# A quantizer's scratch moved into the gate product's PSUM banks, with PSUM split in two pairs and four banks

## The chip, the cores and the metric

The kernel runs on one core of a Trainium2 chip. The metric is the device time of one execution in microseconds, as the median over runs. The engines are named as in the profile: PE is TensorE (matmuls; PEld its weight loads), DVE is VectorE, ACT is ScalarE, POOL is GpSimd, SP is SyncE, which here issues the DMAs. SBUF is the working memory. PSUM is the memory that PE writes to; each of its 128 partitions has eight banks of 512 fp32 numbers.

## The reference

The input is x with four sequences of 2048 tokens and 256 channels; all numbers are fp32. Four layers follow, each added to x behind a layernorm of x:

```python
x = x + attn_a(layernorm(x))   # v times s/s, where s sums exp-features of q and k over a head
x = x + ffn(layernorm(x))
x = x + attn_b(layernorm(x))   # linear attention over the four sequences, unit-norm q and k, two gates
x = x + ffn(layernorm(x))      # the same FFN weights again

def fp4_quant_dequant(x):      # blocks of 16 along the last dim
    scale = max(max(abs(xb)) / 6, 1e-12)
    q = GRID[searchsorted(MID, abs(xb / scale))] * sign(xb) * scale   # 0 .5 1 1.5 2 3 4 6

def ffn(x):                    # w_gate, w_up: 704 x 256; w_down: 256 x 704
    xq = quant(x)
    h = silu(xq @ quant(w_gate).T) * (xq @ quant(w_up).T)
    return quant(h) @ quant(w_down).T
```

Attention A divides q and k by norms over the whole tensor, so sums over all of x are needed before any of its output is final.

## The kernel before

**Staging.** A first pass loads x, sums its Gram matrix on PE, and folds, centers, quantizes and transposes the weights. Then come 16 groups (`group(j)`), each of 128 positions in all four sequences, S = 4 tiles of 128 tokens. A group passes through attention A, the first FFN, attention B and the second FFN. Groups overlap: while one is in an FFN, others are in an attention.

**One FFN tile** (`ffn_tile`, 16 x 2 x 4 = 128 of them). PE makes gate and up products of the tile in two halves of 352 columns (L1448), each product in a bank of its own. ACT takes silu of the gate bank into the SBUF tile `sil` (L1469), and DVE multiplies with the up bank into `h` in SBUF (L1480). Then the inner quantizer `to_grid` runs: DVE takes block maxima and their reciprocals (`to_scales`, L384 and L385), DVE divides by scales (`over_scales`, L389, a first pass over 704 columns, into `qa`), ACT takes scaled absolute values (`to_steps`, L395, into the bf16 tile `qm`), and DVE makes two more passes (`to_sum`, L402, in `qa`; `from_sum`, L405, into `qm`). Meanwhile PE transposes the block maxima (L1287), ACT scales them into `sT` (L1295), and SP spreads them by six DMAs over the partitions of `hqT` (L1304). PE transposes `qm` (L1505), ACT copies the result back (L1516), and POOL multiplies it into `hqT` (L1524). PE makes the down product (L1561), which DVE adds to x (L336 or L1593). The last group's second FFN (`apart` false) applies the scales on POOL to `qa` before the transpose instead (L1271, L1538, L1550).

**Other users of PSUM.** `turn` transposes through a bank (L1155, drained by ACT at L1162); `project` fills a bank for attention A (drained by DVE, L1330) and for attention B (L1178, drained by ACT, L1656); the first pass uses banks for `fold`, `center`, the Gram sums (two banks, L575) and the transposes of weights (L805, L837).

**Order.** `Plan` takes each operation with an engine, a cost, a rank and the tiles that it reads and writes, and lays all of them in one static order: at every step the free engine takes the ready operation of lowest rank whose buffers can be had. `plan.buf("mm")` asks for any free tile of a pool; a tile is held from the operation that first touches it until the last one that does. Engines then run their instructions in that order, and wait for each other by semaphores. The rank of an operation is an offset written beside it plus an entry of `BEGIN`, a table of 16 groups by six stages: attention A, first FFN's input and tiles, attention B, second FFN's input and tiles. `port=True` tells the planner to keep DVE and POOL operations so marked apart. `order(seed)` adds a random number to every rank unless the seed is 0.

```python
plan.pool("mm", banks[:4])      # gate and up products; in the first pass folds, centers, sums
plan.pool("bank", banks[4:])    # all else
tiles("qa", 3, [P, FF], fp)     # the quantizer's fp32 scratch
```

Of the kernel before, what the change touches and what calls it, by code (L numbers as in the profile page):

```python
# [13 lines left out]
AF = mybir.ActivationFunctionType  # L14
# [4 lines left out]
P = 128  # L19
# [230 lines left out]
def kernel(  # L250
# [40 lines left out]
    def one(shape, name, pool=wp, dtype=F32):  # L291
        return pool.tile(shape, dtype, tag=name, name=name)

    banks = [one([P, 512], f"bank{i}", ps) for i in range(8)]
    xs_of = [one([P, S, D], f"x{i}", fp) for i in range(8)]


# [84 lines left out]
    def to_scales(src, amax, rs):  # L382

        nc.vector.tensor_reduce(amax, src, AX.X, ALU.max, apply_absolute_value=True)  # L384
        nc.vector.reciprocal(rs, amax)  # L385

    def over_scales(a, src, rs):

        nc.vector.scalar_tensor_tensor(  # L389
            blocks(a), over_blocks(rs), -6.0 * BELOW, src, ALU.mult, ALU.mult  # L390
        )

    def to_steps(m, a):

        nc.scalar.activation(m, a, AF.Abs, scale=UP)  # L395
# [5 lines left out]
    def to_sum(a, m):  # L401
        nc.vector.scalar_tensor_tensor(a, m, FLOOR, a, ALU.max, ALU.add)  # L402
# [9 lines left out]
    def tiles(name, n, shape, pool, dtype=F32):  # L412
        made = [one(shape, f"{name}{i}", pool, dtype) for i in range(n)]
        plan.pool(name, made)
        return made

    plan.pool("mm", banks[:4])
    plan.pool("bank", banks[4:])
    plan.pool("x", xs_of)
    tiles("turned", 6, [P, KC, GT], fp)  # L420

# [3 lines left out]
    tiles("qmx", 1, [P, S * D], fp, BF16)  # L425
    tiles("sx", 2, [P, 3, S * D // BLK], fp)
    tiles("sil", 2, [P, HF], fp)
    tiles("qa", 3, [P, FF], fp)

    tiles("qm", 4, [P, 6 * P], fp, BF16)  # L430

# [18 lines left out]
    def first_pass():  # L450
# [444 lines left out]

        def fold(at, dst, token, lhs):

            mm = plan.buf("mm")

            def pe():  # L900
                for c in range(KC):
                    nc.tensor.matmul(
                        mm.ap[:, c * P : (c + 1) * P],
                        lhs(c),
                        mapT[:, c, :],
                        start=True,
                        stop=True,
                    )

            op(  # L910
                "PE",
                0.6,
                at,
                pe,
                [(MAPT, 0), (WNAT, 0), (MK, "b")],
                [(mm, 0)],
            )
            op(
                "ACT",
                0.4,  # L920
                at + 1,
                lambda: nc.scalar.copy(dst, mm.ap[:, :D]),
                [(mm, 0)],
                [token],
            )

        def center(at, w, n, tokens, bias=None):

            mm = plan.buf("mm")

            def pe():
                for c in range(KC):
                    nc.tensor.matmul(
                        mm.ap[:, :n], ones, w[:, c, :], start=(c == 0), stop=(c == KC - 1)
                    )

            def dve():
                less, part = mm.ap[:, :n], -1.0 / D  # L940
                if bias:
                    less, part = bias[0], 1.0 / D
                    nc.vector.scalar_tensor_tensor(
                        less, mm.ap[:, :n], -1.0, less, ALU.mult, ALU.add
                    )
                for c in range(KC):
                    nc.vector.scalar_tensor_tensor(
                        w[:, c, :], less, part, w[:, c, :], ALU.mult, ALU.add
                    )

            op("PE", 0.2 + n / 290.0, at, pe, tokens, [(mm, 0)])
            us = 0.3 + n / 300.0 if bias else 0.2 + n / 450.0
            more = [(bias[1], 0)] if bias else []
            op("DVE", us, at + 2, dve, [(mm, 0)], tokens + more, port=bool(bias))
# [64 lines left out]
            "DVE", 0.3, FIRST + 1.0, take_sums, [(b, 0) for b in GRAM] + [("cross", 0)], [("part", 1)]  # L1019
        )  # L1020
        for c in range(KC):
            mm = plan.buf("mm")

            def weigh(c=c, mm=mm):
                if c == 0:
                    nc.tensor.matmul(mm.ap, g00, wqkA[:, 0, :], start=True, stop=True)
                else:
                    nc.tensor.matmul(mm.ap, g01, wqkA[:, 0, :], start=True, stop=False)
                    nc.tensor.matmul(mm.ap, g11, wqkA[:, 1, :], start=False, stop=True)

            op("PE", 1.0 + 0.9 * c, FIRST, weigh, [(G, c), (WQK, 0)], [(mm, 0)])

            def square(c=c, mm=mm):
                for t in range(2):
                    cols = slice(t * D, (t + 1) * D)
                    nc.vector.scalar_tensor_tensor(
                        prod[:, c, cols],
                        mm.ap[:, cols],
                        1.0,
                        wqkA[:, c, cols],  # L1040
                        ALU.mult,
                        ALU.mult,
                        accum_out=part[:, 3 + c, t : t + 1],
                    )

            op(
                "DVE", 0.95, FIRST, square, [(mm, 0), (WQK, 0)], [(PROD, c), ("part", 2 + c)]
            )

        tot = plan.buf("mm")  # L1050

        def total():
            for i in range(5):
# [55 lines left out]


    BEGIN = [
        (-203, -171, -228, -523, -223, -182),
        (30, 31, 72, 172, 140, 266),
        (171, 285, 220, 271, 350, 410),
        (190, 259, 249, 359, 435, 433),
        (280, 328, 329, 443, 489, 531),
        (307, 307, 368, 481, 553, 554),
        (401, 391, 470, 576, 469, 654),
        (518, 526, 518, 624, 554, 722),
        (558, 601, 599, 701, 465, 825),  # L1120
        (552, 581, 635, 689, 613, 817),
        (646, 729, 663, 820, 279, 916),
        (670, 507, 738, 839, 676, 977),
        (741, 808, 767, 897, 501, 969),
        (773, 805, 838, 931, 446, 1029),
        (844, 848, 859, 963, 879, 1776),
        (857, 886, 876, 1038, 88, 801),
    ]

    def group(j):  # L1130
# [304 lines left out]


        def ffn_tile(at, k, s, xqT):
            h, qa, qm, sh = (plan.buf(p) for p in ("h", "qa", "qm", "sh"))

            apart = (k, j) != (2, NJ - 1)  # L1440
            for half in range(2):
                cols = slice(half * HF, (half + 1) * HF)
                g, u, sil = plan.buf("mm"), plan.buf("mm"), plan.buf("sil")

                def hidden(g=g, u=u, cols=cols):
                    for bank, w in ((g, wgT), (u, wuT)):
                        for c in range(KC):
                            nc.tensor.matmul(  # L1448
                                bank.ap[:, :HF],
                                xqT.ap[:, c, s * P : (s + 1) * P],  # L1450
                                w[:, c, cols],
                                start=(c == 0),
                                stop=(c == KC - 1),
                            )

                op(
                    "PE",
                    2.38,
                    at + 2.4 * half,
                    hidden,  # L1460
                    [(xqT, 0), (xqT, 1)]
                    + [("wgu", i) for i in range(3 * half, 3 * half + 3)],
                    [(g, 0), (u, 0), (h, "place", half)],
                )
                op(
                    "ACT",
                    0.42,
                    at + 2.5 + 2.4 * half,
                    lambda g=g, sil=sil: nc.scalar.activation(  # L1469
                        sil.ap, g.ap[:, :HF], AF.Silu  # L1470
                    ),
                    [(g, 0)],
                    [(sil, 0)],
                    table="silu",
                )
                op(
                    "DVE",
                    0.44,
                    at + 3 + 2.4 * half,
                    lambda u=u, sil=sil, half=half: nc.vector.tensor_mul(  # L1480
                        h.ap[:, half * FB // 2 : (half + 1) * FB // 2, :BLK],
                        blocks(sil.ap),
                        blocks(u.ap[:, :HF]),
                    ),
                    [(u, 0), (sil, 0)],
                    [(h, half)],
                )
            to_grid(
                at + 6,
                h,  # L1490
                range(2),
                qa,
                qm,
                sh,
                {"amax": 1.32, "pass": 0.86, "abs": 0.74, "n": FF},
                qm if apart else None,
            )
            hqT = plan.buf("hqT")
            if apart:
# [333 lines left out]

    for j in range(NJ):
        group(j)
    order = plan.order(10)
    with tc.manual_schedule():
        for i in order:
            plan.ops[i]["fn"]()
# [56 lines left out]
```

## Time and profile before

| | |
|---|---|
| Time, median of 3 runs | 1520.65 us (1520.2 to 1521.12) |
| Profiled execution: its own time, given as the span from first to last instruction | 1516.3 us |
| What the median has beyond that span | 4.35 us |
| Instructions | 21213 |
| Granted TensorE clock, mean | 0.998 |
| Gate and up matmuls (L1448) | 2048, busy 641.3 us |
| Down matmuls (L1561) | 1536, busy 351.0 us |
| First and last hidden matmul (L1448) | 113.0 us, 1497.6 us |

The profile is of one execution. A group's line gives the source line, the engine, the operation, what is written and read, the count, the busy time and the mean duration of one, and behind the bar the idle time of the engine ahead of them with what ended most of it. In the timeline a line gives start, length, engine, line, operation and tiles; what stands in brackets is idle time and its releaser. Each fp32 matmul of the program shows as two records.

### The profile page before, as it was taken

To read this page: it belongs to the slowest core of one execution; us is meant where nothing else is said; L and a number is where in the kernel's file an instruction comes from. 1 tells how busy PE (TensorE), PEld (TensorE's weight loads), DVE (VectorE), ACT (ScalarE), POOL (GpSimd) and SP (SyncE) were. 2 spreads that over 40 slices of the span, in tenths; PEclk is the share of its full clock that TensorE was granted. 3 is DMA by queue.
4 is the path that set the end of the run, shared out by engine and by line. 5 is a ranking of instruction groups with operands and counts; after the bars stand their busy time and mean duration, and the time that the engine had idled before them with its cause. 6 is when DMAs were issued, how large, how long until landed. Compare 5 with 4: busy or idle time off the path is not lost.

```text
span 1516.3 us, 21213 instructions
## 1 busy us (share of the span) xinstructions
PE 1480.2 (98%) x6486; PEld 1041.9 (69%) x6486; DVE 1388.9 (92%) x2140; ACT 882.5 (58%) x1812; POOL 747.5 (49%) x782
## 2 busy tenths in 40 slices
PE   7989999999999999999999999999999999999999
PEld 6746666676767667767666666676666776677766
DVE  7899999989999999999999899899889998999986
ACT  6557666466646654654565755675566546565442
POOL 5344454364655445454354554643465435764532
PEclk9999999999999999999999999999999999999999
DMA  9302220222221122213222212122213131122221
GB/s 284 84 1 38 36 41 11 51 59 38 41 58 37 35 53 52 56 34 62 60 43 45 46 25 50 38 46 60 46 19 57 36 61 30 36 52 50 60 61 29
DMA packets 130226, 76.62 MB, mean 51 GB/s; under 512 B 9536, under 2 KB 129856, under 8 KB 130112
## 3 DMA queue, kind: packets, MB, share of 16 engines
q1 hardware_dynamic: 130112, 75.27, 24.2%
q8 instruction: 51, 0.84, 0.2%
q14 instruction: 63, 0.52, 0.1%
HBM read 18.09 MB, written 8.39 MB: 17 GB/s over the span
## 4 chain that ended last, share of the span: by engine, by line
PE 79%; DVE 13%; ACT 3%; issue 2%; DMA 2%; POOL 1%; SPq 0%; ACTq 0%; POOLq 0%; DVEq 0%
PE bank L1448 33%; PE bank L1561 19%; PE bank L1178 16%; PE bank L1155 4%; PE bank L575 3%; PE bank L1505 2%; DMA hqT<-sT 1%; DVE qa L389 1%; DVE qa L402 1%; DVE sh L384 1%; DVE h L1480 1%; DVE x L336 1%; DVE pp L1668 1%; DVE qm L405 1%; PE bank L1287 1%
## 5 line engine op out<-in xcount | busy, mean ns | idle before, releaser
L1448 PE MATMUL bank<-wguT,turned 128*128 128x352 f32 x2048 | 641.3, 461 | 0.8 <-DVE h L1480 0.8
L1448 PEld LDWEIGHTS bank<-wguT,turned 128*128 128x128 f32 x2048 | 378.6, 191 | 193.3 <-issue 11.7
L1524 POOL TENSOR_TENSOR hqT<-hqT,qm 128x768 f32<-128x768 f32 x124 | 223.9, 1810 | 332.1 <-ACT qm L1516 163.8
L1561 PE MATMUL bank<-wdT,hqT 128*128 128x256 f32 x1536 | 351.0, 380 | 3.1 <-POOL hqT L1524 2.2
L1561 PEld LDWEIGHTS bank<-wdT,hqT 128*128 128x128 f32 x1536 | 289.5, 190 | 61.1 <-issue 7.9
L395 ACT ACTIVATE qm<-qa 128x704 bf16<-128x704 f32 (+1 forms) x136 | 105.7, 782 | 115.0 <-DVE qa L389 103.5
L1469 ACT ACTIVATE sil<-bank 128x352 f32<-128x352 f32 x256 | 116.0, 457 | 70.3 <-PE bank L1448 64.1
L1480 DVE TENSOR_TENSOR h<-sil,bank 128x352 f32<-128x352 f32 x256 | 128.5, 509 | 21.7 <-ACT sil L1469 11.0
L402 DVE SCALAR_TENSOR_TENSOR qa<-qm,qa 128x704 f32<-128x704 bf16 (+2 forms) x136 | 139.0, 1022 | 9.9 <-ACT qm L395 9.8
L1776 POOL TENSOR_TENSOR pp<-vg,sc 128x1024 f32<-128x1024 f32 x64 | 133.1, 2095 | 22.9 <-DVE tok L1797 19.7
L389 DVE SCALAR_TENSOR_TENSOR qa<-sh,h 128x704 f32<-128x704 f32 x128 | 137.6, 1083 | 0.9
L405 DVE SCALAR_TENSOR_TENSOR qm<-qm,qa 128x704 bf16<-128x704 bf16 x124 | 129.8, 1048 | 4.4 <-POOL norms_f L363 0.5
L1516 ACT COPY qm<-bank 128x768 bf16<-128x768 bf16 x124 | 98.1, 795 | 59.3 <-PE bank L1505 56.7
L384 DVE TENSOR_REDUCE sh<-h 128x44 f32<-128x748 f32 x128 | 119.2, 931 | 4.2
L1271 POOL TENSOR_TENSOR qax<-qax,sx 128x1024 f32<-128x1024 f32 x32 | 71.4, 2231 | 100.6 <-DVE qax L405 74.7
L1178 PE MATMUL bank<-wqkB,turned 128*128 128x512 f32 x256 | 120.0, 595 | 0.8 <-ACT turned L1162 0.8
L1178 PE MATMUL bank<-wvz,turned 128*128 128x512 f32 x256 | 116.8, 595 | 1.7 <-ACT wdT L846 0.9
L1162 ACT COPY turned<-bank 128x512 f32<-128x512 f32 x160 | 87.2, 589 | 43.1 <-PE bank L1155 42.7
L1668 DVE TENSOR_TENSOR pp<-qk 128x1024 f32<-128x1024 f32 x64 | 81.8, 1279 | 7.1 <-ACT qk L1656 7.0
L342 ACT ACTIVATE dev<-x,norms_f 128x256 f32<-128x256 f32 x128 | 64.9, 507 | 29.8 <-DVE x L336 27.8
L1178 PEld LDWEIGHTS bank<-wvz,turned 128*128 128x128 f32 x256 | 46.7, 190 | 49.4 <-issue 42.7
L1675 DVE TENSOR_REDUCE sc<-pp 128x64 f32<-128x1024 f32 x64 | 77.8, 1215 | 1.3
(195 smaller groups left out, 2211.9 us busy)
## 6 DMA issues: line engine op xcount, KB each, us to landing
hqT<-sT SPq DMA_DIRECT2D x744, 64.0 KB
x<-in_L_attn_a_x_dram SPq DMA_DIRECT2D x23, 512.0 KB
out_dram<-x SPq DMA_DIRECT2D x64, 128.0 KB
hqT<-in_L_ffn_w_down_dram SPq DMA_DIRECT2D x2, 352.0 KB
hqT<-in_L_ffn_w_gate_dram SPq DMA_DIRECT2D x5, 128.0 KB
hqT<-in_L_ffn_w_up_dram SPq DMA_DIRECT2D x5, 128.0 KB
x<-in_L_attn_a_x_dram SPq DMA_DIRECT2D x4, 128.0 KB
pp<-in_L_attn_a_Wq_dram SPq DMA_DIRECT2D x2, 256.0 KB
```

The costliest lines, as they stand in the source:

```text
L384: nc.vector.tensor_reduce(amax, src, AX.X, ALU.max, apply_absolute_value=True)
L389: nc.vector.scalar_tensor_tensor(blocks(a), over_blocks(rs), -6.0 * BELOW, src, ALU.mult, ALU.mult)
L395: nc.scalar.activation(m, a, AF.Abs, scale=UP)
L402: nc.vector.scalar_tensor_tensor(a, m, FLOOR, a, ALU.max, ALU.add)
L405: nc.vector.scalar_tensor_tensor(a if to is None else to, m, FLOOR, a, ALU.max, ALU.subtract)
L1178: nc.tensor.matmul(bank.ap[:, :n], lhs.ap[:, c, s * P : (s + 1) * P], w[:, c, :], start=(c == 0), stop=(c == KC - 1),)
L1448: nc.tensor.matmul(bank.ap[:, :HF], xqT.ap[:, c, s * P : (s + 1) * P], w[:, c, cols], start=(c == 0), stop=(c == KC - 1),)
L1469: lambda g=g, sil=sil: nc.scalar.activation(sil.ap, g.ap[:, :HF], AF.Silu),
L1480: lambda u=u, sil=sil, half=half: nc.vector.tensor_mul(h.ap[:, half * FB // 2 : (half + 1) * FB // 2, :BLK], blocks(sil.ap), blocks(u.ap[: ...
L1524: lambda: nc.gpsimd.tensor_mul(hqT.ap, hqT.ap, qm.ap.rearrange("p (c n) -> p c n", n=P)),
L1561: nc.tensor.matmul(o.ap[:, :D], hqT.ap[:, i, :], wdT[:, i, :], start=(i == 0), stop=(i == 5),)
L1776: nc.gpsimd.tensor_mul(pv.ap.rearrange("p t (n e) -> p t n e", e=HD), vg.ap[:, :, :D].rearrange("p t (n e) -> p t n e", e=HD), over_blocks ...
```

## The change

PSUM is divided anew: two pairs of adjacent banks (`pair`) and four single banks (`bank`); the pool `mm` is gone. A tile's two gate halves go to the two banks of one pair. Its up halves, and what else used `mm`, go to the four single banks. The inner quantizer no longer calls `to_grid`: it has its own copies of the same five steps, which use the pair as scratch in place of `qa` (704 columns across both banks, and 44 for the reciprocals), so the pair is held until `from_sum`. Those DVE operations are no longer marked `port`. `qa` falls from three tiles to two; in the groups only the last group's second FFN still uses it. The table of ranks is new, and the order is taken without random numbers. No arithmetic instruction is added or removed.

```diff
@@ -291,7 +291,8 @@
     def one(shape, name, pool=wp, dtype=F32):
         return pool.tile(shape, dtype, tag=name, name=name)
 
-    banks = [one([P, 512], f"bank{i}", ps) for i in range(8)]
+    pairs = [one([P, 2, 512], f"pair{i}", ps) for i in range(2)]
+    banks = [one([P, 512], f"bank{i}", ps) for i in range(4)]
     xs_of = [one([P, S, D], f"x{i}", fp) for i in range(8)]
 
 
@@ -414,8 +415,8 @@
         plan.pool(name, made)
         return made
 
-    plan.pool("mm", banks[:4])
-    plan.pool("bank", banks[4:])
+    plan.pool("pair", pairs)
+    plan.pool("bank", banks)
     plan.pool("x", xs_of)
     tiles("turned", 6, [P, KC, GT], fp)
 
@@ -425,7 +426,7 @@
     tiles("qmx", 1, [P, S * D], fp, BF16)
     tiles("sx", 2, [P, 3, S * D // BLK], fp)
     tiles("sil", 2, [P, HF], fp)
-    tiles("qa", 3, [P, FF], fp)
+    tiles("qa", 2, [P, FF], fp)
 
     tiles("qm", 4, [P, 6 * P], fp, BF16)
 
@@ -895,7 +896,7 @@
 
         def fold(at, dst, token, lhs):
 
-            mm = plan.buf("mm")
+            mm = plan.buf("bank")
 
             def pe():
                 for c in range(KC):
@@ -928,7 +929,7 @@
 
 
 
-            mm = plan.buf("mm")
+            mm = plan.buf("bank")
 
             def pe():
                 for c in range(KC):
@@ -1019,7 +1020,7 @@
             "DVE", 0.3, FIRST + 1.0, take_sums, [(b, 0) for b in GRAM] + [("cross", 0)], [("part", 1)]
         )
         for c in range(KC):
-            mm = plan.buf("mm")
+            mm = plan.buf("bank")
 
             def weigh(c=c, mm=mm):
                 if c == 0:
@@ -1047,7 +1048,7 @@
                 "DVE", 0.95, FIRST, square, [(mm, 0), (WQK, 0)], [(PROD, c), ("part", 2 + c)]
             )
 
-        tot = plan.buf("mm")
+        tot = plan.buf("bank")
 
         def total():
             for i in range(5):
@@ -1109,22 +1110,22 @@
 
 
     BEGIN = [
-        (-203, -171, -228, -523, -223, -182),
-        (30, 31, 72, 172, 140, 266),
...
-        (844, 848, 859, 963, 879, 1776),
-        (857, 886, 876, 1038, 88, 801),
+        (-765, -488, -607, -512, -538, -479),
+        (50, -442, -240, 262, -219, 287),
...
+        (836, 812, 859, 960, 1010, 1933),
+        (863, 308, 878, 1046, 300, 567),
     ]
 
     def group(j):
@@ -1435,18 +1436,19 @@
 
 
         def ffn_tile(at, k, s, xqT):
-            h, qa, qm, sh = (plan.buf(p) for p in ("h", "qa", "qm", "sh"))
+            h, g, qm, sh = (plan.buf(p) for p in ("h", "pair", "qm", "sh"))
+            qa = plan.buf("qa") if (k, j) == (2, NJ - 1) else None
 
             apart = (k, j) != (2, NJ - 1)
             for half in range(2):
                 cols = slice(half * HF, (half + 1) * HF)
-                g, u, sil = plan.buf("mm"), plan.buf("mm"), plan.buf("sil")
-
-                def hidden(g=g, u=u, cols=cols):
-                    for bank, w in ((g, wgT), (u, wuT)):
+                u, sil = plan.buf("bank"), plan.buf("sil")
+
+                def hidden(u=u, cols=cols, half=half):
+                    for bank, w in ((g.ap[:, half], wgT), (u.ap, wuT)):
                         for c in range(KC):
                             nc.tensor.matmul(
-                                bank.ap[:, :HF],
+                                bank[:, :HF],
                                 xqT.ap[:, c, s * P : (s + 1) * P],
                                 w[:, c, cols],
                                 start=(c == 0),
@@ -1460,16 +1462,16 @@
                     hidden,
                     [(xqT, 0), (xqT, 1)]
                     + [("wgu", i) for i in range(3 * half, 3 * half + 3)],
-                    [(g, 0), (u, 0), (h, "place", half)],
+                    [(g, half), (u, 0), (h, "place", half)],
                 )
                 op(
                     "ACT",
                     0.42,
                     at + 2.5 + 2.4 * half,
-                    lambda g=g, sil=sil: nc.scalar.activation(
-                        sil.ap, g.ap[:, :HF], AF.Silu
+                    lambda sil=sil, half=half: nc.scalar.activation(
+                        sil.ap, g.ap[:, half, :HF], AF.Silu
                     ),
-                    [(g, 0)],
+                    [(g, half)],
                     [(sil, 0)],
                     table="silu",
                 )
@@ -1485,15 +1487,52 @@
                     [(u, 0), (sil, 0)],
                     [(h, half)],
                 )
-            to_grid(
+            def flat():
+                return g.ap.rearrange("p t n -> p (t n)")
+
+            def a_and_m():
+                return flat()[:, :FF], qm.ap[:, :FF]
+
+            def rs():
+                return flat()[:, FF : FF + FB]
+
+            def hidden_scales():
+                to_scales(h.ap, sh.ap[:, 0, :], rs())
+
+            def hidden_over_scales():
+                over_scales(flat()[:, :FF], h.ap[:, :, :BLK], rs())
+
+            op(
+                "DVE",
+                1.32,
                 at + 6,
-                h,
-                range(2),
-                qa,
-                qm,
-                sh,
-                {"amax": 1.32, "pass": 0.86, "abs": 0.74, "n": FF},
-                qm if apart else None,
+                hidden_scales,
+                [(h, 0), (h, 1)],
+                [(sh, 0), (g, 0), (g, 1)],
+            )
+            op(
+                "DVE", 0.88, at + 7, hidden_over_scales, [(h, 0), (h, 1)], [(g, 0), (g, 1)]
+            )
+
+            def hidden_steps():
+                a, m = a_and_m()
+                to_steps(m, a)
+
+            def hidden_grid():
+                a, m = a_and_m()
+                from_sum(a, m, m if apart else qa.ap)
+
+            op("ACT", 0.74, at + 8, hidden_steps, [(g, 0), (g, 1)], [(qm, 0)])
+            op(
+                "DVE", 0.88, at + 10, lambda: to_sum(*a_and_m()), [(qm, 0)], [(g, 0), (g, 1)]
+            )
+            op(
+                "DVE",
+                0.88,
+                at + 10.1,
+                hidden_grid,
+                [(g, 0), (g, 1)] + ([] if apart else [(qm, 0)]),
+                [(qm if apart else qa, 0)],
             )
             hqT = plan.buf("hqT")
             if apart:
@@ -1833,7 +1872,7 @@
 
     for j in range(NJ):
         group(j)
-    order = plan.order(10)
+    order = plan.order(0)
     with tc.manual_schedule():
         for i in order:
             plan.ops[i]["fn"]()
```

More of the change, by code (lines that the diff above doesn't have):

```diff
@@ L1111 @@
     BEGIN = [
-        (-203, -171, -228, -523, -223, -182),
-        (30, 31, 72, 172, 140, 266),
[L1114 to L1125, printed above, removed]
-        (844, 848, 859, 963, 879, 1776),
-        (857, 886, 876, 1038, 88, 801),
+        (-765, -488, -607, -512, -538, -479),
+        (50, -442, -240, 262, -219, 287),
+        (183, 283, 216, 300, -429, 413),
+        (182, -98, 227, 358, 290, 440),
+        (269, 382, 228, 444, 501, 531),
+        (359, -27, 367, 453, 551, 553),
+        (413, 440, 467, 576, 644, 647),
+        (515, 301, 519, 290, 467, 728),
+        (559, 607, 599, 662, 614, 826),
+        (556, 583, 635, 683, -236, 818),
+        (643, 734, 655, 1018, -402, 221),
+        (676, -469, 747, 850, 844, 988),
+        (740, 743, 773, 899, 300, 972),
+        (772, 773, 840, 931, -244, 1033),
+        (836, 812, 859, 960, 1010, 1933),
+        (863, 308, 878, 1046, 300, 567),
     ]
```

## Prediction

> **What bounds the kernel now.** I read the page's busy shares first, to see which engines have room.
>
> ```profile
> span 1516.3 us, 21213 instructions
> PE 1480.2 (98%) x6486; PEld 1041.9 (69%) x6486; DVE 1388.9 (92%) x2140; ACT 882.5 (58%) x1812; POOL 747.5 (49%) x782
> ```
>
> PE has nearly no idle time and DVE little; ACT and POOL are half empty. A busy PE hides small gaps, so I went to the trace's matmuls and took the interval from each start to the next. Summing, over all shapes, the lower quartile of a shape's interval (295 ns for the 128x352 hidden matmul, 215 ns for 128x256, 429 ns for 128x512, 55 ns for a bf16 transpose) gives 1454.8 us, PE's issue floor. The excess over it is 49.2 us. With 9.2 us before the first matmul and 3.5 us behind the last start that makes the span, to a few tenths. By hundreds of us the excess is 6.3, 9.2, 2.9, 3.3, 2.9, 1.1, 1.4, 2.0, 3.0, 5.7, 0.8, 2.6, 1.2, 0.9, 5.3 and 0.7. So **at most 49 us (3.2%) can be gained by any reordering**, and a quiet stretch already loses only about 1 us in 100.
>
> Next, the windows view: the middle and the end of the span.
>
> ```profile
> 1200.00:1450.00 250.00, 249.47 (x1106) 179.76 (x1105) 233.37 (x333) 132.77 (x267) 124.16 (x102) 1.00 0.25 48
> 1450.00:1516.00 66.00, 59.52 (x278) 45.02 (x276) 47.79 (x68) 24.55 (x52) 21.11 (x18) 1.00 0.17 40
> ```
>
> The columns are stretch, length, then busy us of PE, PEld, DVE, ACT and POOL, granted clock (full) and DMA. PE is saturated late in the middle and not in the tail.
>
> Then the groups of instructions: the quantizer's three passes over the hidden tile, and GpSimd's multiplication.
>
> ```profile
> L402 DVE SCALAR_TENSOR_TENSOR qa<-qm,qa 128x704 f32<-128x704 bf16 (+2 forms) x136 | 139.0, 1022 | 9.9 <-ACT qm L395 9.8
> L389 DVE SCALAR_TENSOR_TENSOR qa<-sh,h 128x704 f32<-128x704 f32 x128 | 137.6, 1083 | 0.9
> L405 DVE SCALAR_TENSOR_TENSOR qm<-qm,qa 128x704 bf16<-128x704 bf16 x124 | 129.8, 1048 | 4.4 <-POOL norms_f L363 0.5
> L1524 POOL TENSOR_TENSOR hqT<-hqT,qm 128x768 f32<-128x768 f32 x124 | 223.9, 1810 | 332.1 <-ACT qm L1516 163.8
> ```
>
> The means hide two populations. The medians are 884, 886 and 892 ns, the longest 2.6 us. Sorted by whether a GpSimd instruction ran beside them, the passes average 871, 885 and 888 ns alone, and 1183, 1321 and 1249 ns beside one. The timeline near the end shows what that does to PE:
>
> ```profile
> 1456.06 3.89 POOL L1524 TENSOR_TENSOR hqT<-hqT,qm 128x768 f32<-128x768 f32 x2
> 1456.13 2.32 DVE L402 SCALAR_TENSOR_TENSOR qa<-qm,qa 128x704 f32<-128x704 bf16 x1 [1.33 <-ACT qm L395]
> 1458.48 2.21 DVE L405 SCALAR_TENSOR_TENSOR qm<-qm,qa 128x704 bf16<-128x704 bf16 x1
> 1460.75 0.51 PE L1505 MATMUL bank<-ident,qm 128*128 128x128 bf16 x6 [1.70 <-DVE qm L405]
> ```
>
> Two passes that take 0.88 us alone took 4.5 together beside GpSimd, and PE sat idle 1.70 us behind them. The rows with one operand in PSUM do not stretch: the 256 products h<-sil,bank never exceed 524 ns, and average 508 ns beside GpSimd against 514 alone.
>
> **The change, part by part.**
>
> *1. The three passes move to a PSUM pair.* Each then has one SBUF and one PSUM input, like h<-sil,bank. Taken at their time alone they save 128 x (1083 - 885) = 25.3 us, 128 x (1040 - 884) = 20.0 us (1040 is the mean of the 704-wide form) and 124 x (1048 - 888) = 19.8 us: **65 us of DVE**, from 1389 to 1324 (92% to 87%). No row of this trace writes PSUM from DVE, so I bound the price of the three passes and the reciprocal, four instructions a tile. From above: vz<-bank,norms_a,bvz at 512 elements takes 727 ns against 682 for pp<-pp alone, 45 ns more; 128 x 4 x 45 = 23 us. From below: behind x<-x,bank at 256 the next DVE instruction starts after 331 ns, behind tok<-pp after 342 (medians where DVE did not wait); 11 ns less, a gain of 6 us. I take zero: h<-sil,bank at 515 ns lies on the line through the SBUF-only rows (417 at 256 elements, 682 at 512, hence 516 at 352), and it is the nearest row.
>
> [...]
>
> *2. ACT and GpSimd.* The step pass (L395, 790 ns from SBUF) reads PSUM instead. L1516 copies 768 elements from PSUM in 795 ns, per element 729 ns for 704: between 0 and -8 us of ACT in all; I take zero, since ACT is at 58%. GpSimd's multiplication has a median of 1647 ns against its mean of 1810, so up to 124 x 0.163 = 20 us of GpSimd time goes too. Neither is on the path by itself; if their cover went, those sums are what they would give or cost.
>
> *3. PSUM is split anew.* Up products (u), and the first pass's folds, centers and sums, go to the four general banks. From first matmul to end of drain, what uses those banks now adds up to 373 us of transposes, 346 of attention A, 293 of Q, K, V and gates, 201 of scales, 222 of hidden transposes and 709 of down and output projections: 2144 us, over some 1400 us 1.5 banks of four. The u halves add 256 x 5.7 = 1459 us: 2.6 of four. That leaves room on average, less in bursts.
>
> [...]
>
> *4. The pair is held longer than a bank was.* Today a gate bank is free after silu, 3.1 us on average from its first matmul. Now the pair stays taken to the end of from_sum. Pairing the n-th tile's first hidden matmul with the n-th from_sum, I find today 10.7 us at the least, 26.7 at the median and 27.6 on average, with one tile every 10.84 us. So 2.5 tiles are in flight, and two will be allowed. In 96 of 126 cases tile n+2 starts today before tile n's from_sum has ended. Queued behind such a wait on PE is everything that comes after the hidden matmuls; for that reason the order has to change, and the new ranks do that. The sum for one undisturbed tile is 4.78 (PE) + 0.46 + 0.51 + 0.93 + 0.43 + 0.88 + 0.79 + 0.88 + 0.88 = 10.5 us, which agrees with the 10.7; the other 17 us are queueing on DVE. They must fall under 21.7 - 10.5 = 11.2 us. With 65 us less in DVE's queue, and PE able to take projections and down products in between (as much of PE as the hidden matmuls), I take it that they do.
>
> *5. First pass.* The Gram sums hold two of the four general banks, so folds and centers turn over in two instead of six; PE is covered there by the Gram matmuls (40.15 us busy in the first 50). Two qa tiles instead of three serve eight weight quantizations; their last gate/up transposes end at 93.2 us and the first hidden matmul starts at 113.0, so about 20 us cover it. I cost both at zero; without that cover 0 to +5 us.
>
> *6. Ranks and seed.* No arithmetic instruction is added or dropped; everything is reordered, ACT's 58 table loads of 1.28 us (74 us, on an engine at 58%) with it. Only the excess can change.
>
> **The sum, against the span.** In the twelve hundreds from 200 to 1400 us the excess is 27.8; the five quiet ones average 1.1. With DVE less late the others should come close to that: 12 x 1.1 = 13, hence -14.6. The tail (5.3 + 0.7) holds the 1.70 us above: -2. The start (15.5) stays, at +2 for part 5. Together -14.6: span 1502, and with the 4.35 us between span and median (1520.65 - 1516.3) **1506 us**. Its own range: half of the middle's recovery, 1513; all of it, with half of start and tail (10.7), 1495.
>
> A measurement of this kernel can tell about 0.2%, 3 us, from no change: below 1517.6 is faster, above 1523.7 slower.
>
> **Rivals.**
>
> *A, slower: the pairs pace PE.* If the wait for a pair stays above 21.7 us, the tile period grows by half the excess: 127 x 0.5 x 0.1 = 6 us for each 0.1 us. It speaks for it that today's mean is 27.6; against it, that 17 us of that are queueing which the order can shorten. Point of decision: from_sum of tile n against the first hidden matmul of tile n+2. At 22.1 us: +25, 1546; I put it at 1525 to 1580.
>
> *B, no change:* PE is at its floor in the middle and the losses at start and tail (21.5 us) do not hang on the passes; what DVE gains turns into idle DVE. For: 0.7 to 1.4 us per 100 where it is quiet. Then 1518 to 1523, likeliest 1520.
>
> *C, the change doesn't do what it says:* the passes still stretch beside GpSimd, or each PSUM instruction costs 45 ns more, while two tiles in flight remain. DVE stays at 1389 or above, the excess rises by a third: +16, 1537. Against it: 203 products beside GpSimd, none stretched.
>
> **How the numbers follow.** Forecast 0.64, A 0.22, B 0.09, C 0.05. Faster 0.64, same 0.09, slower 0.27. The range reaches down a little under the forecast's own low end, to 1491, and up through B and C into the nearer half of A, to 1545.
>
> **What would show it.** Right: the three passes at 0.8 to 0.95 us mean with a maximum near the mean; DVE near 1324 us; hold of a pair under 21 us; PE's excess between 200 and 1400 us below 20. Wrong: PE waiting before L1448's successor on from_sum, or on the u product, for more than 10 us in all; passes over 1 us; a first hidden matmul later than 118 us.

## The result, and the profile after

The changed kernel takes 1544.59 us (median of 4 runs, 1543.54 to 1545.69) against 1520.43: **slower by 1.55%**, ratio 1.0155, 95% interval 1.014 to 1.0169. The forecast was 1506 and faster. The span grew from 1516.3 to 1542.7 us, by 26.4.

The page's head and the groups that answer to those of before:

```profile
span 1542.7 us, 21190 instructions
PE 1497.5 (97%) x6486; PEld 1041.0 (67%) x6486; DVE 1313.9 (85%) x2140; ACT 879.4 (57%) x1811; POOL 676.9 (44%) x782
L1563 POOL TENSOR_TENSOR hqT<-hqT,qm 128x768 f32<-128x768 f32 x124 | 214.8, 1734 | 343.4 <-DMA hqT<-sT 180.8
L403 DVE SCALAR_TENSOR_TENSOR pair<-qm,pair 128x704 f32<-128x704 bf16 x128 | 113.7, 888 | 25.1 <-ACT qm L396 23.8
L390 DVE SCALAR_TENSOR_TENSOR pair<-pair,h 128x704 f32<-128x704 f32 x128 | 114.6, 896 | 3.2
L406 DVE SCALAR_TENSOR_TENSOR qm<-qm,pair 128x704 bf16<-128x704 bf16 x124 | 109.6, 885 | 6.2
```

The three passes of the hidden tile no longer stretch: the longest are 900, 897 and 889 ns (2.6 us before), and beside GpSimd they average the same as alone (896, 887 and 885 ns). DVE lost 75 us of work, and the kernel became slower. The windows that stood for the saturated middle and the tail:

```profile
1200.00:1450.00 250.00, 245.51 (x1101) 176.28 (x1100) 219.47 (x340) 139.45 (x291) 115.02 (x119) 1.00 0.22 43
1450.00:1543.00 93.00, 87.84 (x393) 64.27 (x391) 63.12 (x98) 34.23 (x74) 22.90 (x21) 1.00 0.25 52
```

PE was busy 249.47 of 250 us in the first of them, now 245.51, while DVE fell from 233 to 219. **Both engines are idle more than before.** The rows of DVE's waits add up to 198 us (101 before), 105 of them for ACT (47) and 78 for PE (39). The largest, in the view of who waited for whom (total us, times, longest):

```profile
DVE h L1482 <- ACT sil L1471: 39.3, 36, 3.4
DVE pair L403 <- ACT qm L396: 23.8, 37, 1.7
DVE x L1632 <- PE bank L1600: 21.7, 13, 5.1
DVE h L1482 <- PE bank L1450: 18.6, 16, 3.1
DVE x L337 <- PE bank L1600: 17.4, 17, 3.8
```

Before, the first and the third stood at:

```profile
DVE h L1480 <- ACT sil L1469: 11.0, 14, 1.7
DVE x L1593 <- PE bank L1561: 12.1, 11, 3.8
```

PE's waits are small and spread over many places, in all 40 us against 33 before, and the pair has hardly a share:

```profile
PE bank L1600 <- POOL hqT L1563: 6.7, 7, 2.3
PE pair L1450 <- ACT sil L1471: 2.5, 4, 1.4
PE bank L1544 <- DVE qm L406: 2.3, 4, 1.1
PE pair L1450 <- DVE qm L406: 1.4, 4, 0.5
```

By the prediction's own measure, the excess of the intervals between matmul starts over their lower quartile, PE's excess went from 49.2 to 73.3 us: 15.5 to 21.9 before 200 us, 27.8 to 45.8 between 200 and 1400, 6.0 to 5.7 after. These 24 us are nearly all of the span's 26.4. Of PE's waits in the view, those behind its first matmul grew from 23 to 33 us; the rest of the 24 lies in gaps too short for that view and in slower stretches, and what ended these was not worked out. One of the longer places, from the timeline:

```profile
1039.01 2.75 PE L1600 MATMUL bank<-wdT,hqT 128*128 128x256 f32 x12
1041.67 2.30 POOL L1563 TENSOR_TENSOR hqT<-hqT,qm 128x768 f32<-128x768 f32 x1 [4.28 <-DMA hqT<-sT]
1044.03 4.54 PE L1600 MATMUL bank<-wdT,hqT 128*128 128x256 f32 x12 [2.27 <-POOL hqT L1563]
```

GpSimd waited for the DMAs that spread a tile's scales; the down product was next in PE's static order, and PE stood 2.27 us although it was not short of work in total.

The place cost more than these 2.27 us. From 1044.8 to 1048.2 us the granted clock was 0.50, and the twelve matmuls took 4.54 us where the same product at 1039.01 took 2.75. In its span the changed kernel has four such stretches of 3.41 us, each beside a gap of PE of 1.5 to 2.6 us; the kernel before has two, beside gaps of 3.1 and 3.6 us. (Not every gap has one: that of 1.7 us at 457 us does not.) Half of their length is 6.8 us now and 3.4 before, so by this estimate up to 3.4 of the 24 us are a lower clock.

The pair does what was asked of it: the time from a tile's first hidden matmul to the end of its from_sum fell from 27.6 to 15.8 us on average (10.6 at the least). Before, tile n+2 began ahead of tile n's from_sum in 96 of 126 cases; now in none, and in 42 of 126 it begins within 1.5 us of it. The order keeps close to the pairs, with little reserve.

### The profile page after: what moved, and what is told of

Same layout as the page of the kernel before. It is cut to its first block, busy times and chain, and to the rows that moved or that the text cites. A ratio compares the mean times of both kernels' runs of the same rounds, so it can differ in the third digit from the quotient of the medians.

```text
span 1542.7 us, 21190 instructions
## 1 busy us (share of the span) xinstructions
PE 1497.5 (97%) x6486; PEld 1041.0 (67%) x6486; DVE 1313.9 (85%) x2140; ACT 879.4 (57%) x1811; POOL 676.9 (44%) x782
## 4 chain that ended last, share of the span: by engine, by line
PE 67%; DVE 18%; ACT 5%; DMA 4%; issue 3%; POOL 3%; SPq 0%; ACTq 0%; POOLq 0%; DVEq 0%
PE bank L1600 17%; PE bank L1179 16%; PE pair L1450 14%; PE bank L1450 13%; PE bank L1156 3%; DMA hqT<-sT 3%; PE bank L576 2%; DVE sh L385 2%; PE bank L1544 2%; DVE h L1482 2%; DVE pair L403 2%; POOL hqT L1563 1%; DVE pp L1707 1%; DVE pair L390 1%; DVE sc L1714 1%
## 5 line engine op out<-in xcount | busy, mean ns | idle before, releaser
L1563 POOL TENSOR_TENSOR hqT<-hqT,qm 128x768 f32<-128x768 f32 x124 | 214.8, 1734 | 343.4 <-DMA hqT<-sT 180.8
L1450 PE MATMUL pair<-wguT,turned 128*128 128x352 f32 x1024 | 350.8, 465 | 4.1 <-ACT sil L1471 2.5
L1450 PE MATMUL bank<-wguT,turned 128*128 128x352 f32 x1024 | 345.5, 460 | 0.5 <-DVE h L1482 0.5
L1450 PEld LDWEIGHTS bank<-wguT,turned 128*128 128x128 f32 x1024 | 194.9, 190 | 109.9 <-DVE h L1482 1.1
L1450 PEld LDWEIGHTS pair<-wguT,turned 128*128 128x128 f32 x1024 | 184.6, 191 | 91.2 <-issue 9.2
L1471 ACT ACTIVATE sil<-pair 128x352 f32<-128x352 f32 x256 | 114.3, 458 | 120.2 <-PE pair L1450 113.8
L396 ACT ACTIVATE qm<-pair 128x704 bf16<-128x704 f32 x128 | 96.6, 755 | 105.4 <-DVE pair L390 95.5
L1815 POOL TENSOR_TENSOR pp<-vg,sc 128x1024 f32<-128x1024 f32 x64 | 123.4, 1945 | 31.0 <-DVE tok L1836 28.2
L403 DVE SCALAR_TENSOR_TENSOR pair<-qm,pair 128x704 f32<-128x704 bf16 x128 | 113.7, 888 | 25.1 <-ACT qm L396 23.8
L390 DVE SCALAR_TENSOR_TENSOR pair<-pair,h 128x704 f32<-128x704 f32 x128 | 114.6, 896 | 3.2
L406 DVE SCALAR_TENSOR_TENSOR qm<-qm,pair 128x704 bf16<-128x704 bf16 x124 | 109.6, 885 | 6.2
```

What stands on the lines that cost most here:

```text
L390: nc.vector.scalar_tensor_tensor(blocks(a), over_blocks(rs), -6.0 * BELOW, src, ALU.mult, ALU.mult)
L406: nc.vector.scalar_tensor_tensor(a if to is None else to, m, FLOOR, a, ALU.max, ALU.subtract)
L1450: nc.tensor.matmul(bank[:, :HF], xqT.ap[:, c, s * P : (s + 1) * P], w[:, c, cols], start=(c == 0), stop=(c == KC - 1),)
L1471: lambda sil=sil, half=half: nc.scalar.activation(sil.ap, g.ap[:, half, :HF], AF.Silu),
L1563: lambda: nc.gpsimd.tensor_mul(hqT.ap, hqT.ap, qm.ap.rearrange("p (c n) -> p c n", n=P)),
L1815: nc.gpsimd.tensor_mul(pv.ap.rearrange("p t (n e) -> p t n e", e=HD), vg.ap[:, :, :D].rearrange("p t (n e) -> p t n e", e=HD), over_blocks ...
```

## Experiments

Two theories at first. **O:** banks are scarce, so worse orders are all that can be laid, and the loss sits in the order. **W:** PE stands at run time for a pair. A third, **T**, blames the new ranks alone. Times are medians against the kernel before on the same chip (1519.8 to 1521.1). The edits are shown abridged.

**Four kernels that take the change apart, mostly under before's ranks and seed.** e1 is the changed kernel with them:

```diff
-    BEGIN = [(-765, -488, ...), ...]     plan.order(0)
+    BEGIN = [(-203, -171, ...), ...]     plan.order(10)
```

> The changed kernel with the table of ranks and the seed of the kernel before. Theory O (the pairs are scarce, so what is lost lies in the order that can be laid, and ranks made for the new layout win part of it back): clearly slower than the changed kernel, 1575 to 1610 us. Theory W (PE stands at run time waiting for a pair, whatever the order): within 10 us of the changed kernel's 1545. Theory T (the layout is good, the new ranks are bad): 1525 us or less.

1593.6 us, ratio 1.0483 (1.0465 to 1.0501). Under ranks that were not made for it the layout loses 73 us; the new ranks win back 49 of them. T falls, and W with it, since the order matters.

e2 splits PSUM only:

```diff
-    g, u, sil = plan.buf("mm"), plan.buf("mm"), plan.buf("sil")   # and to_grid on qa
+    g = plan.buf("pair"); u = plan.buf("bank")                     # to_grid on qa, as before
```

> Ranks and seed of before; PSUM split in two pairs and four banks, the up product in the four banks, but the quantizer's scratch in SBUF as before and the pair free again after silu. Theory O with the up product in the general banks as the larger part: near e1, 1570 to 1600 us. Theory O with the hold as the larger part: 1525 to 1550 us. Theory T: within 5 us of before, 1520.

1599.6 us, 1.0516 (1.0496 to 1.0537). **The split alone costs 79 us**, as the first form of O had it, with nothing held for the quantizer and DVE's passes in SBUF as before.

e3 adds the hold, in the order alone:

```diff
-    [(a, 0), (m, 0)], [(to or a, 0)],                    # from_sum, reads and writes
+    [(a, 0), (m, 0)], [(to or a, 0), (g, 0), (g, 1)],    # the planner keeps the pair taken
```

> As e2, but the order keeps the pair taken until from_sum, as if the scratch lay in it; the passes still run in SBUF beside GpSimd. Theory O with the hold as a large part: 50 to 110 us slower than e2, 1640 to 1700, and slower than e1 by what the passes in PSUM are worth. Theory W or T: within 15 us of e2.

1705.9 us, 1.1216 (1.119 to 1.1243), 106 above e2 as expected, and a little over the 1700 that was named. Against e1, which has the same split, hold, ranks and seed, the passes in PSUM are worth 112 us here. That price has two parts that were not told apart: e3's passes still stretch, and its order still keeps them apart from GpSimd (`port`), which e1's does not.

e4 keeps the changed kernel's order of instructions and puts the scratch back in SBUF:

```diff
-    return g.ap.rearrange("p t n -> p (t n)")    # scratch; tokens of the pair stay for the order
+    return qa.ap                                  # reciprocals in sh.ap[:, 2, :]
```

> The changed kernel's order of all instructions, unchanged, but the quantizer's scratch in SBUF: at run time the pair is free after silu, and the passes can stretch beside GpSimd again. Theory O: no faster than the changed kernel; the passes' stretch comes back, 1548 to 1570 us. Theory W: the waits for pairs go, 1515 to 1538 us.

1662.3 us, 1.0932 (1.0908 to 1.0956). No theory had this size. The pair is free after silu at run time, and no gain shows; but the stretch came back in the same run, so what speaks most plainly against W is that PE waits only 1.4 us behind from_sum in the changed kernel. The group of the third pass:

```profile
L406 DVE SCALAR_TENSOR_TENSOR qm<-qm,qa 128x704 bf16<-128x704 bf16 x124 | 157.9, 1275 | 6.2
```

885 ns became 1275, 890 alone and 1562 beside GpSimd. 133 us more of DVE work in the same order (1447.4 against 1313.9) cost 118 us. That order was laid without keeping DVE and GpSimd apart, so this is the price of the stretch in an order that does not expect it.

So, at before's ranks: +79 (split) +106 (hold) -112 (passes) = +73, and -49 from the new ranks makes +24, the result. The middle two depend on the path: e1, which has both, is 6 us below e2, which has neither, so at these ranks the split alone is as large as the whole loss. A part of the larger steps is the clock: its mean was 0.969 in e3's profiled execution, 0.990 in e1 and e2, 0.985 in e4 and 0.996 in the changed kernel. As an estimate, by span times what is missing to 1, that is up to 37 us of the 106, 37 of the 112 and 19 of e4's 118.

**What makes the split dear?** e6 is the kernel before with one edit:

```diff
-    g, u, sil = plan.buf("mm"), plan.buf("mm"), plan.buf("sil")
+    g, u, sil = plan.buf("mm"), plan.buf("bank"), plan.buf("sil")
```

> The kernel before, ranks and seed too, with one edit: the up product comes from the four general banks, while the gate product keeps the other four single banks to itself; the scratch stays in SBUF. If the squeeze of the up product makes e2's loss: 1580 to 1600 us, near e2's 1600. If the two-bank unit of the pair makes it: 1520 to 1540 us.

1576.6 us, 1.0373 (1.0358 to 1.0388): 57 of the 79 us. It came out a little under the expected range, but far from the other one. The up product crowds the banks that transposes, projections and down products need. PE had the same matmuls and, with this edit, fewer places for their results: its excess went from 49.2 to 107.4 us. Its busy time hides a part of that; it grew from 1480.2 to 1500.8 us for the same work. The other 22 us of the split were not taken apart.

e5 gives the scratch a pair of its own and leaves six single banks to everything else, under before's ranks and seed:

```diff
+    pairs = [one([P, 2, 512], f"pair{i}", ps) for i in range(1)]   # from block maxima to from_sum
+    banks = [one([P, 512], f"bank{i}", ps) for i in range(6)]      # all products and transposes
```

> Ranks and seed of before. One pair only, taken by a tile from its block maxima to from_sum and by nothing else; gate and up products and all other work share six single banks. The passes run in PSUM as in the changed kernel. Theory O1 (what costs is that the product banks are tied: gate banks through the quantizer, the up product squeezed into four): most of the loss of e1 goes, 1530 to 1560 us against e1's 1594. Theory O2 (any scratch in PSUM costs, since two of eight banks are gone for products): 1585 us or more.

1534.9 us, 1.0091 (1.007 to 1.0112), against e1's 1593.6. Most of e1's loss comes from tying up the product banks, and not from scratch in PSUM as such; some 15 us stay.

e12 takes the passes out of e5 and leaves the two banks idle:

```diff
-    banks = [one([P, 512], f"bank{i}", ps) for i in range(8)]      # against the kernel before
+    banks = [one([P, 512], f"bank{i}", ps) for i in range(6)]
-    plan.pool("mm", banks[:4])
-    plan.pool("bank", banks[4:])
+    plan.pool("bank", banks)                                       # scratch in qa, passes marked port
```

> As e5 (ranks and seed of before, six single banks for all products and transposes), but the other two banks lie idle: the scratch stays in SBUF, and the order keeps DVE and GpSimd apart as before. Against e5 this is what the passes in PSUM are worth where the order was laid for their lock. If they are worth what e4 and e3 suggest, about 110 us: 1630 us or more. If that was the worth under a short hold alone: 5 to 30 us above e5's 1535, 1540 to 1565.

1562.0 us, 1.0269 (1.0255 to 1.0283). In this layout, against an order laid for the stretch, the passes in PSUM are worth 27 us, not 112. Two banks fewer, with the two pools made one, cost 41 us (1562 against 1521), and the passes give 27 of them back.

**How much of the result is one order's luck?** e7 is the kernel before with `plan.order(3)` in place of `plan.order(10)`:

> The kernel before with another seed (3 in place of 10) and nothing else: another order of the same instructions in the same layout. If an order only counts by its seed's luck on the chip: anywhere from 1520 to 1550 us. If the layout of before is forgiving, a second order costs little: 1522 to 1532 us.

1531.4 us, 1.0076 (1.0061 to 1.0091): within the range expected of a forgiving layout, but 11.6 us are half of the change's loss. Then the same kind of random search over ranks, of similar length, for three layouts. It moved entries of `BEGIN` and added a shift for each tile, and kept what shortened the program's own plan of the order (e8 also has another seed, 328):

```diff
-    ffn_tile(24.0 * s, k, s, xqT)
+    ffn_tile(24.0 * s + SHIFT[j][k - 1][s], k, s, xqT)    # and a searched BEGIN
```

e8 and e11 are the layout of e5, e9 that of before, e10 that of the changed kernel.

> The layout of e5 (one pair for the scratch alone, six banks for the rest) with ranks searched for it, from the table of before. Theory L (the passes in PSUM are worth it where the product banks stay free): faster than before, 1503 to 1517 us. Theory N (PE is at its floor, the order decides within a few us, the passes are worth nothing): 1517 to 1526 us.

> As e8, from another start of the search, without random numbers in the ranks. Shows how far two orders of one layout lie apart: within 8 us of e8, and by theory L below 1520 us.

> The layout of before with the same search as long, from its own table. Theory L: 1513 to 1521 us, a few us above e8. Theory N: the same as e8 within 5 us.

> The changed kernel with the same search as long, from its own table. If its ranks were merely not searched far enough: 1525 us or less. If the layout limits what an order can reach: 1535 to 1546 us.

| Kernel | us | ratio to before, 95% |
|---|---|---|
| e8, one pair, searched | 1514.05 | 0.9951 (0.9938 to 0.9964) |
| e11, one pair, second search | 1522.03 | 1.0016 (1.0005 to 1.0027) |
| e9, layout of before, searched | 1532.78 | 1.0072 (1.0058 to 1.0086) |
| e10, changed kernel, searched | 1541.81 | 1.014 (1.0123 to 1.0157) |

e8 is faster than both kernels. e10 stays where the changed kernel was, so this search did not mend its layout. e9 is slower than the kernel it started from: theory L and theory N both missed it. A search that made e9 slower is no proof that no ranks would mend the changed layout. With e7, e9 says that the order of before is some 11 to 13 us better on the chip than two siblings in its layout. Measured against those siblings (1531 to 1533), the changed layout costs 9 to 13 us (1541.8 and 1544.6), and, as far as two siblings can tell, **about half of the 24 us is that before's order is an uncommonly good one**. Against the same siblings the one-pair layout with the passes in PSUM is 9 to 19 us faster (e8 and e11): there the freed DVE did pay. What makes one order fall behind on the chip and not its sibling was not settled: the gaps are many and short. e11 beside e8 is 8 us apart, the most that was expected, and lies above theory L's bound of 1520; a single pair of orders decides nothing below that.

The head of e8's profile, and its waits of PE for GpSimd:

```profile
span 1512.4 us, 21285 instructions
PE 1480.4 (98%) x6486; PEld 1040.8 (69%) x6486; DVE 1315.5 (87%) x2140; ACT 880.9 (58%) x1812; POOL 676.1 (45%) x782
L403 DVE SCALAR_TENSOR_TENSOR pair<-qm,pair 128x704 f32<-128x704 bf16 x128 | 113.9, 890 | 24.5 <-ACT qm L396 23.6
PE bank L1620 <- POOL hqT L1583: 8.3, 11, 1.8
```

DVE has the changed kernel's load (1315.5 against 1313.9) and PE is as busy as before (98%). In e8 56 of 126 tiles begin before the from_sum of two tiles earlier, in the changed kernel none; its excess is 42.9 us.

## Why the prediction was wrong, step by step

- **The passes (step 1): right.** 896, 888 and 885 ns against 885, 884 and 888 taken; DVE at 1313.9 against 1324, the other 10 us mostly because operations such as pp<-pp stretch less beside GpSimd (52 us in all, 62 before; 906 ns on average beside it, 1238 before). The 871 and 1183 ns named for to_sum mix in narrower rows of the weights; at 704 columns it took 879 alone and 1211 beside GpSimd, which changes no term. The price of PSUM taken at zero held: alone, over_scales rose by 11 ns, to_sum's median by 5, from_sum fell by 3 and the reciprocal rose from 428 to 436, some 21 ns or 3 us for 128 tiles. That lies between the bounds of -6 and +23 us.
- **ACT and GpSimd (step 2):** 755 ns for the step pass from PSUM, inside the bounds. GpSimd's multiplication fell to a mean of 1734 ns only; the bound was 1647.
- **The split of PSUM (step 3): wrong, and the first cause.** 2.6 of four banks on average was called room enough and costed at zero; the crowding alone costs 57 us at before's ranks (e6), the whole split 79 (e2). The mean said nothing of the bursts, and the sentence that named them gave them no price.
- **The hold (step 4): the size right, its price missed.** 15.8 us, far below the 21.7 needed. Rival A's price was a wait at run time, and that is 1.4 us behind from_sum. The cost that the runs show is one of order: an order laid so that no third tile comes in costs 106 us at before's ranks while the passes stay in SBUF (e3). With the passes in PSUM too, hold and passes together came to 6 us less than the split alone (e1, e2), so what the hold costs in the changed kernel itself stays open.
- **The first pass (step 5): right** as to the first hidden matmul, 112.9 us against 113.0; the excess up to 200 us rose by 6.4 where 2 were allowed, up to 3.4 of that by two more stretches at half clock.
- **The ranks and the sum (step 6): wrong.** "With DVE less late the others should come close to that" took DVE's load for the reason of PE's gaps. DVE's load fell by more than was forecast, and the excess in the middle rose from 27.8 to 45.8 where 13 was expected. It also took the order as something that any table would reach again, while before's was better than two siblings (e7, e9).
- **The signs:** those for being right came, but for one: passes under 0.95 us, DVE near 1324, the hold under 21. None of those for being wrong came. Only PE's excess, 45.8 where under 20 was named, told that the forecast failed.
- **The rivals:** A has the sign and the size (1525 to 1580, and 1546 at a hold of 22.1 us), and the size by luck: the hold was 15.8 us, under the 21.7 where A's wait begins. Half of its reason is right: two tiles in flight, but paid in the order. The stated range just holds 1544.6, through A's part of it and not the forecast's. B and C fell: the stretch is gone, and the kernel did not stay where it was.

## What to carry to other kernels

Before moving scratch into PSUM, count the banks that stay for the matmuls' results, by bursts and not by the mean; a product bank held as scratch through a long DVE chain takes freedom from PE's order, which need not show in any single wait (here 106 us in e3, and 1.4 us of waits behind from_sum in the changed kernel). When a kernel with a hand-made order changes its resources, separate layout from order: run the old ranks in the new layout, and a sibling order in the old one, before a difference of 1% is put down to either. Before an engine's saved load is counted as saved time, look whether the engine that sets the time waits for that load: 75 us less on DVE went with 26 us more of span here.

## What was not expected of the hardware

A DVE pass over 704 columns that reads or writes a region across two PSUM banks, with another operand in SBUF, took 885 to 896 ns, within 11 ns of the same pass in SBUF alone (879 to 888), and as much beside GpSimd (885 to 896). The passes in SBUF took 0.3 to 0.7 us more on average beside GpSimd: 1211 to 1321 ns in the kernel before, and 1562 against 890 for from_sum in e4. Being rid of this, and of the order that allows for it, was worth 27 us in one layout and 112 in another; bringing it back into an unchanged order cost 118.
